# A loop over runs of an expert layer: two wide blocks for three narrow ones, and semaphores set back in stages

## The chip, the cores and the metric

The kernel runs on one core of one Trainium2 chip. A core has five engines with instruction streams of their own: TensorE (PE: matmuls, with its weight loads listed as PEld), VectorE (DVE), ScalarE (ACT), GpSimd (POOL, which here issues the indirect DMAs) and SyncE (SP, which issues the other DMAs). They wait for one another and for DMAs through semaphores. Matmuls read the on-chip memory SBUF and write PSUM, a small memory from which DVE and ACT read the results. The metric is the device time of one execution, in microseconds (us); less is better. Times of the kernel before: median 9008.61 us of 3 runs, from 9005.31 to 9009.49.

## The reference

`x` is (4, 1024, 1024) f32, that is 4096 tokens of 1024 numbers. Two residual stages follow each other. The second holds nearly all the time: a layer of 8 experts, of which every token uses the two that a router gives the highest probability.

```python
x = x + xattn(layernorm(x), ctx_512, W_k, b_k, ln_gamma, ln_beta)   # cross-attention, softmax weights
x = x + ffn(layernorm(x), gate_w, w1, w2, w3)

def ffn(x, gate_w, w1, w2, w3):            # E=8, D=1024, M=3584
    x_flat = x.reshape(-1, d)
    router_probs = softmax(x_flat @ gate_w)
    topk_w, topk_idx = top_k(router_probs, 2);  topk_w /= sum(topk_w)
    x_rep_sort = take(x_flat, argsort(topk_idx.reshape(-1)) // 2)
    group_sizes = bincount(topk_idx, length=8)
    h = silu(ragged_dot(x_rep_sort, w1, group_sizes)) * ragged_dot(x_rep_sort, w3, group_sizes)
    out_sort = ragged_dot(h, w2, group_sizes)
    # back to the order of the tokens, weighted with topk_w and summed over the two
```

With the inputs given, the router sends 984, 991, 1080, 994, 1047, 1004, 1046 and 1046 tokens to the eight experts, 8192 in all. The kernel learns these numbers only while it runs.

## The kernel before

A first stage works through the tokens in tiles of 128: attention, layer norms, router. It writes the normalised tokens to `h_d` and the first residual sum to `out` in device memory, and enters each token into the slot table `id_d` of its two experts. Then it counts: the table RUNS holds the cases that the code has been built for, a number of blocks and their width, such as `(3, 352)` for up to 1056 tokens in three blocks of 352. Small DVE operations (L523 to L564) pick for every expert the first case that holds its tokens and fill `run_e`, `run_s` and `run_k` (expert, first slot, case) and `run_n` (number of runs).

The loop `tc.For_i(0, n_run)` (L896) makes one run at a time: here eight, one for each expert. SP loads the run's expert and first slot into registers, every engine loads its case, and `tc.Switch` (L900) branches to the code of that case. At the end of an iteration all engines stop, the semaphores are set back, and the next iteration begins.

Within `run`, a block of `width` tokens goes through two phases, both by a scheme of Strassen and Winograd: seven products of half-size factors in place of eight. So a matmul has n = width/2 moving columns.

- Phase 1: for 14 pairs of column tiles of w1 and w3, load a tile (L600, 1 MB), form three sums and one difference of its quarters on DVE (`weight_sums`, L632 to L635), 28 matmuls (L825), and `combine` (L666 to L672), which adds the seven products together out of PSUM. Then `silu` (L836), the product of both (L837) into `g`, and `token_sums` (L650 to L652), which adds the sums T1 to T4 that phase 2 needs, so that `g` has seven parts for each of 14 steps.
- Phase 2: for four quarters `q` of the output columns, load w2 in units of 8, 8, 6 and 6 tiles, sum them, and make 14×7 matmuls (L864) that accumulate in PSUM; `combine` puts the result into `y`.

That is 14×2×28 + 4×98 = 1176 matmuls for a block. The order of TensorE is that of the source (`manual_schedule`); the other engines' instructions are ordered by the scheduler.

Small work is put between the matmuls through the list `late`, from which one step is taken after every group in phase 1 and after every seven matmuls in phase 2. `tokens_out` transposes a piece of `y` (L774), adds it, weighted, to `acc` (L776), and after the last quarter scatters `acc` to `out` (L780); what is left of the last quarter of a run is done in the next run, or behind the loop (`leftover`). `tokens_in` transposes the next block's tokens (L743) into `x` (copies L749, L751). The rows are gathered by indirect DMAs (L699): `rows` from `h_d`, `acc` from `out`. `load_first` brings the next run's first tiles of w1 and w3 into tiles of their own (`w1a`, `w3a`), at the start of the last block's phase 2.

Weight tiles rotate through three buffers (`wp`). In PSUM, `banks()` takes four of six rotating buffers for the seven products of a group, and the transposes rotate through two more. There are three row tiles of 128 tokens (RT = 3), each with a tile in `rows` and one in `acc`.

Of the kernel before, what the change touches and what calls it, by code (L numbers as in the profile page):

```python
# [22 lines left out]
RUNS = [(1, 192), (1, 376), (2, 288), (2, 376), (3, 288)]  # L23
RUNS += [(3, w) for w in range(320, 377, 8)]
# [10 lines left out]
def kernel(  # L35
# [540 lines left out]
    with ExitStack() as st:  # L576
        fst = st.enter_context(tc.tile_pool(name="fst", bufs=1))
        wp = st.enter_context(tc.tile_pool(name="wp", bufs=3))
        hp = st.enter_context(tc.tile_pool(name="hp", bufs=1))
        gp = st.enter_context(tc.tile_pool(name="gp", bufs=2))  # L580
        ip = st.enter_context(tc.tile_pool(name="ip", bufs=2))
        ps = st.enter_context(tc.tile_pool(name="ps", bufs=6, space=PSUM))
        pst = st.enter_context(tc.tile_pool(name="pst", bufs=2, space=PSUM))
# [4 lines left out]
        W2K = [8, 8, 6, 6]  # L588
# [3 lines left out]
        XW = RT * P  # L592
        assert all(w // 2 <= NM and w <= XW for _, w in RUNS)


        T1, B11, B12, B21, B22, T2, T4 = range(7)
        T3 = B12
# [9 lines left out]
        def load(wf, ex, k0, kn, c0):  # L607
            t = wp.tile([P, KD, QW], F32, tag="w", name="wt")
            weights(t, wf, ex, k0, kn, c0)
            return t  # L610

        def factors(t, kn, halves, s):

            n = kn // 2
            if halves:
                v = t[:, :kn, :].rearrange("p (i h) c -> p i h c", h=2)
                lo, hi = v[:, :, 0, :], v[:, :, 1, :]
            else:
                lo, hi = t[:, :n, :], t[:, n:kn, :]
            s1, s2, s4 = (s[:, j, :n, :] for j in range(3))  # L620

            return dict(
                p1=lo[:, :, :P], p2=hi[:, :, :P], p3=s4, p4=hi[:, :, P:], p5=s1, p6=s2,
                p7=lo[:, :, P:],
            )

        def weight_sums(t, kn, halves, s=None):
            if s is None:
                s = wp.tile([P, 3, HK, P], F32, tag="s", name="ws")
            f = factors(t, kn, halves, s)  # L630
# [4 lines left out]
            nc.vector.tensor_tensor(a21, a11, a21, ALU.subtract)  # L635
            return f

        RIGHT = dict(p1=B11, p2=B21, p3=B22, p4=T4, p5=T1, p6=T2, p7=T3)
        BANK = dict(p1=(0, 0), p2=(1, 0), p6=(1, 1), p5=(2, 0), p7=(2, 1), p3=(3, 0), p4=(3, 1))
        ENDS = ["p1", "p6", "p7", "p4"]  # L640
# [4 lines left out]
        def token_sums(v, n):  # L645

            def two(a, b):
                return v[..., a : b + 1 : b - a, :]

            nc.vector.tensor_tensor(two(T1, T3), two(B12, B22), two(B11, B12), ALU.subtract)  # L650
            nc.vector.tensor_tensor(v[..., T2, :], v[..., B22, :], v[..., T1, :], ALU.subtract)
            nc.vector.tensor_tensor(v[..., T4, :], v[..., B21, :], v[..., T2, :], ALU.subtract)  # L652

        def banks():
            return [ps.tile([P, N], F32, tag="ps", name=f"ps{i}") for i in range(4)]

        def combine(pp, n, c, wide):

            def pair(t):
                return t[:, : 2 * n].rearrange("p (a b) -> p a b", b=n)  # L660

            def twice(v):
# [3 lines left out]
            nc.scalar.copy(p1s, pp[0][:, :n])  # L666
            nc.vector.tensor_tensor(pair(c), pair(pp[1]), twice(p1s), ALU.add)  # L667
            vu = gp.tile([P, 2, n], F32, tag="vu", name="vu")
            nc.vector.tensor_tensor(vu, pair(pp[2]), twice(c[:, n : 2 * n]), ALU.add)  # L669
            mid = c[:, n : 2 * wide - n].rearrange("p (a b) -> p a b", b=wide - n)[:, :, :n]  # L670
            nc.vector.tensor_tensor(mid, pair(pp[3]), vu, ALU.add)  # L671
            nc.vector.tensor_tensor(  # L672
                c[:, wide + n : wide + 2 * n], pp[2][:, :n], vu[:, 1, :], ALU.add
            )

# [32 lines left out]
        rd0 = fst.tile([P, RT], I32, name="rd0")  # L708
        rows = [fst.tile([P, D], F32, name=f"rows{s}") for s in range(RT)]
        w1a = fst.tile([P, KD, QW], F32, name="w1a")  # L710
        w3a = fst.tile([P, KD, QW], F32, name="w3a")
        s1a = fst.tile([P, 3, HK, P], F32, name="s1a")
# [6 lines left out]
        acc = [fst.tile([P, D], F32, name=f"acc{s}") for s in range(RT)]  # L719
        for a in acc:  # L720
            nc.vector.memset(a, 0.0)
# [3 lines left out]
        def load_rows(s0):  # L725
            load_ids(ids0, s0)
            where_from(rd0, ids0)
            for s in range(RT):
                gather(rows[s], h_d, rd0, s, P)

        def load_first(i):
            ex = expert(i)
            load_rows(first_slot(i))
            weights(w1a, w1f, ex, 0, KD, 0)
            weights(w3a, w3f, ex, 0, KD, 0)

        def tokens_in():


            def step(s, h):  # L740
                pt = pst.tile([P, N], F32, tag="pt", name="pt_h")
                for k in range(HK):
                    nc.tensor.transpose(  # L743
                        pt[:, ts(k, P)], rows[s][:, ts(HK * h + k, P)], ident
                    )
                src = pt.rearrange("p (a b) -> p a b", b=P)
                dst = x[:, ds(HK * h, HK), ts(s, P)]
                if h % 2:
                    nc.vector.tensor_copy(dst, src)  # L749
                else:  # L750
                    nc.scalar.copy(dst, src)  # L751
# [14 lines left out]

        def tokens_out(ids, split, q, y):
# [3 lines left out]
            def step(s, r):  # L771
                pt = pst.tile([P, N], F32, tag="pt", name="pt_y")
                for d in range(2):
                    nc.tensor.transpose(pt[:r, ts(d, P)], yv[:, d, ds(s * P, r)], ident)  # L774
                part = acc[s][:r, ts(q, QW)]
                nc.vector.scalar_tensor_tensor(  # L776
                    part, pt[:r, :QW], ids.bitcast(F32)[:r, s, 1:2], part, ALU.mult, ALU.add
                )
                if q == DQ - 1:
# [3 lines left out]
                        in_=acc[s][:r, :],  # L783
# [7 lines left out]
        def leftover():  # L791
            return tokens_out(ids1, [P] * RT, DQ - 1, y1)

        def run(i, ex, s0, blocks, width):
            n = width // 2
            split = [min(P, width - c) for c in range(0, width, P)]

# [9 lines left out]
            for b in range(blocks):  # L807
                ids, rd = take_ids()
                last = b == blocks - 1
                if not last:  # L810
                    load_rows(s0 + (b + 1) * width)
                g = hp.tile([P, NI, 7, n], F32, tag="g", name="g")
                for i2 in range(NI):
                    cs = []
                    for wf, wa, tag in ((w1f, w1a, "c1"), (w3f, w3a, "c3")):
                        t = load(wf, ex, 0, KD, i2 * QW) if b or i2 else wa
                        if t is w1a:
                            left = factors(w1a, KD, False, s1a)
                        else:
                            left = weight_sums(t, KD, False)  # L820
                        pp = banks()
                        for p in ORDER if b or i2 else EARLY:
                            bk, half = BANK[p]
                            for k in range(HK):
                                nc.tensor.matmul(  # L825
                                    pp[bk][:, ts(half, n)], left[p][:, k, :],
                                    right[p][:, k, :],
# [8 lines left out]
                    nc.scalar.activation(c1, c1, AF.Silu)  # L836
                    nc.vector.tensor_tensor(  # L837
                        g[:, i2, B11 : B22 + 1, :].rearrange("p a b -> p (a b)"), c1, c3,
                        ALU.mult,
                    )  # L840
                    token_sums(g[:, i2, :, :], n)

                if last:
                    load_first(i + 1)
# [6 lines left out]
                for s, r in enumerate(split):  # L851
                    gather(acc[s][:r, :], of, rd, s, r)
                for q in range(DQ):
                    pp = banks()
                    i2 = 0
                    for kn in W2K:
                        t = load(w2f, ex, 2 * i2, kn, q * QW)
                        left = weight_sums(t, kn, True)
                        for k in range(kn // 2):
                            for p in ORDER:  # L860
                                bk, half = BANK[p]


                                nc.tensor.matmul(  # L864
                                    pp[bk][:, ts(half, n)], left[p][:, k, :],
                                    g[:, i2, RIGHT[p], :],
                                    start=(i2 == 0 and half == 0),
                                    stop=(i2 == NI - 1 and p in ENDS),
                                )
                            i2 += 1  # L870
                            if late and i2 > 1:
                                late.pop(0)()
                    if last and q == DQ - 1:
# [5 lines left out]
                    if q == 1:  # L879
                        late += tokens_in()  # L880

                        def sums():
                            nonlocal right
                            if last:
                                weight_sums(w1a, KD, False, s1a)
                            else:
                                right = token_factors(n)

                        late.append(sums)

        load_first(0)
        for step in tokens_in():
            step()
        weight_sums(w1a, KD, False, s1a)
        n_run = nc.values_load(run_n, min_val=1, max_val=NRUN)
        with tc.For_i(0, n_run) as i:  # L896
# [36 lines left out]
```

## Time and profile before

| view | value |
| --- | --- |
| median of 3 runs | 9008.61 us |
| profiled execution, own time | 9005.26 us |
| its span, first to last instruction | 9003.5 us |
| mean granted TensorE clock | 0.987 |
| first matmul of the loop | 535.38 us |
| start of the first leftover transpose behind the loop | 8988.21 us |
| DVE busy | 5109.8 us, 57% |
| ACT, POOL busy | 8%, 5% |
| DMA | 1236.38 MB, mean 137 GB/s |

Matmuls and weight loads are listed separately and overlap. A row of the profile's groups gives line, engine, operation, the output and input tiles, the shapes, the number of records, then the busy time and the mean length of one record, then the idle time of the engine before them and what ended it. Because matmuls are pipelined, the mean length of a record is more than the time between the starts of two. Records such as `128x176` name 128 partitions by 176 columns, here n = 176. The forms in the loop are n = 164, 168, 176 and 180, for widths of 328, 336, 352 and 360, in three blocks each. Branches and register loads are in the trace but do not count as busy. Loads of weights land 4.7 us (768 KB) and 5.1 us (1 MB) after their issue, in the median.

### The profile page before, as it was taken

To read this page: it belongs to the slowest core of one execution; us is meant where nothing else is said; L and a number is where in the kernel's file an instruction comes from. 1 tells how busy PE (TensorE), PEld (TensorE's weight loads), DVE (VectorE), ACT (ScalarE), POOL (GpSimd) and SP (SyncE) were. 2 spreads that over 40 slices of the span, in tenths; PEclk is the share of its full clock that TensorE was granted. 3 is DMA by queue.
4 is the path that set the end of the run, shared out by engine and by line. 5 is a ranking of instruction groups with operands and counts; after the bars stand their busy time and mean duration, and the time that the engine had idled before them with its cause. 6 is when DMAs were issued, how large, how long until landed. Compare 5 with 4: busy or idle time off the path is not lost. (4 is left out here: it accounts for less than half of the span.)

```text
span 9003.5 us, 140017 instructions
## 1 busy us (share of the span) xinstructions
PE 8812.5 (98%) x59462; PEld 8651.3 (96%) x59463; DVE 5109.8 (57%) x10101; ACT 698.5 (8%) x1528; POOL 412.4 (5%) x496
## 2 busy tenths in 40 slices
PE   8979999999999999999999999999999999999999
PEld 5579999999999999999999999999999999999999
DVE  5665655655655655556556556456565565555554
ACT  3310000000000000000000000000000000000000
POOL 2310000000000000000000000000000000000000
PEclk9989999999999999999999999999999999999999
DMA  3234444444443444444444434444444444434343
GB/s 139 109 132 145 139 147 146 138 149 136 154 130 120 144 135 139 133 139 141 142 134 143 142 124 137 145 131 151 142 145 133 129 140 137 140 129 144 125 140 126
DMA packets 1115213, 1236.38 MB, mean 137 GB/s; under 512 B 35312, under 2 KB 1075184, under 8 KB 1114416
## 3 DMA queue, kind: packets, MB, share of 16 engines
q1 hardware_dynamic: 1081616, 1118.37, 38.3%
q0 software_dynamic: 32656, 107.24, 3.4%
q8 instruction: 501, 8.21, 0.4%
q14 instruction: 296, 2.42, 0.1%
q10 hardware_dynamic: 144, 0.13, 0.0%
HBM read 1155.26 MB, written 73.53 MB: 136 GB/s over the span
## 5 line engine op out<-in xcount | busy, mean ns | idle before, releaser
L825 PE MATMUL ps<-x,wt 128*128 128x168 f32 (+3 forms) x15744 | 2510.6, 309 | 0.0
L825 PEld LDWEIGHTS ps<-x,wt 128*128 128x128 f32 x15744 | 2351.7, 190 | 0.0
L864 PE MATMUL ps<-g,wt 128*128 128x168 f32 (+3 forms) x10752 | 2070.9, 309 | 0.0
L632 DVE TENSOR_TENSOR ws<-wt 128x512 f32<-128x512 f32 (+1 forms) x1040 | 693.7, 667 | 2120.1 <-DMA wt<-in_L_ffn_w_dram 2042.2
L864 PEld LDWEIGHTS ps<-g,wt 128*128 128x128 f32 x10752 | 1691.4, 190 | 0.0
L825 PE MATMUL ps<-xs,ws 128*128 128x168 f32 (+3 forms) x10624 | 1659.2, 309 | 0.0
L864 PE MATMUL ps<-g,ws 128*128 128x168 f32 (+3 forms) x8064 | 1615.3, 309 | 0.0
L825 PEld LDWEIGHTS ps<-xs,ws 128*128 128x128 f32 x10624 | 1579.0, 190 | 0.0
L864 PEld LDWEIGHTS ps<-g,ws 128*128 128x128 f32 x8064 | 1294.7, 190 | 0.0
L667 DVE TENSOR_TENSOR c<-ps,p1s 128x352 f32<-128x352 f32 (+3 forms) x672 | 346.5, 516 | 1030.9 <-PE ps L825 1000.1
L825 PE MATMUL ps<-x,ws 128*128 128x168 f32 (+3 forms) x5312 | 883.2, 309 | 0.0
L825 PE MATMUL ps<-xs,wt 128*128 128x168 f32 (+3 forms) x5248 | 872.5, 309 | 0.0
L825 PEld LDWEIGHTS ps<-x,ws 128*128 128x128 f32 x5312 | 804.0, 190 | 0.0
L825 PEld LDWEIGHTS ps<-xs,wt 128*128 128x128 f32 x5248 | 794.3, 190 | 0.0
L633 DVE TENSOR_TENSOR ws<-ws,wt 128x512 f32<-128x512 f32 (+1 forms) x1040 | 692.0, 665 | 28.4
L635 DVE TENSOR_TENSOR wt<-wt 128x512 f32<-128x512 f32 (+1 forms) x1040 | 685.7, 659 | 0.0
L634 DVE TENSOR_TENSOR ws<-wt,ws 128x512 f32<-128x512 f32 (+1 forms) x1040 | 684.6, 658 | 0.0
L666 ACT COPY p1s<-ps 128x168 f32<-128x168 f32 (+3 forms) x768 | 228.2, 297 | 4658.8 <-PE ps L864 2341.3
L836 ACT ACTIVATE c<-c 128x672 f32<-128x672 f32 (+3 forms) x336 | 261.5, 778 | 2648.0 <-DVE c L671 2626.8
L671 DVE TENSOR_TENSOR c<-ps,vu 128x352 f32<-128x352 f32 (+3 forms) x672 | 344.6, 513 | 28.5 <-PE ps L825 20.8
L669 DVE TENSOR_TENSOR vu<-ps,c 128x352 f32<-128x352 f32 (+3 forms) x672 | 342.3, 509 | 5.7 <-PE ps L825 5.6
L699 POOL DMA_INDIRECT rows<-h_d,rd x75 | 79.7, 1063 | 4880.1 <-DVE ws L633 2278.0
(186 smaller groups left out, 3746.1 us busy)
## 6 DMA issues: line engine op xcount, KB each, us to landing
wt<-in_L_ffn_w_dram SPq DMA_DIRECT2D x848, 1024.0 KB, 5.1
wt<-in_L_ffn_w_dram SPq DMA_DIRECT2D x192, 768.0 KB, 4.7
xt<-in_x_dram SPq DMA_DIRECT2D x32, 512.0 KB, 4.3
out_dram<-x SPq DMA_DIRECT2D x32, 512.0 KB, 2.9
h_d<-hn SPq DMA_DIRECT2D x32, 512.0 KB, 2.6
w1a<-in_L_ffn_w_dram SPq DMA_DIRECT2D x9, 1024.0 KB
w3a<-in_L_ffn_w_dram SPq DMA_DIRECT2D x9, 1024.0 KB
cx<-in_ctx_dram SPq DMA_DIRECT2D x4, 1024.0 KB
```

The costliest lines, as they stand in the source:

```text
L632: nc.vector.tensor_tensor(f["p5"], a21, a22, ALU.add)
L633: nc.vector.tensor_tensor(f["p6"], f["p5"], a11, ALU.subtract)
L634: nc.vector.tensor_tensor(f["p3"], a12, f["p6"], ALU.subtract)
L635: nc.vector.tensor_tensor(a21, a11, a21, ALU.subtract)
L666: nc.scalar.copy(p1s, pp[0][:, :n])
L667: nc.vector.tensor_tensor(pair(c), pair(pp[1]), twice(p1s), ALU.add)
L669: nc.vector.tensor_tensor(vu, pair(pp[2]), twice(c[:, n : 2 * n]), ALU.add)
L671: nc.vector.tensor_tensor(mid, pair(pp[3]), vu, ALU.add)
L699: nc.gpsimd.indirect_dma_start(out=dst, out_offset=None, in_=src, in_offset=bass.IndirectOffsetOnAxis(ap=rd[:n, s : s + 1], axis=0),)
L825: nc.tensor.matmul(pp[bk][:, ts(half, n)], left[p][:, k, :], right[p][:, k, :], start=(k == 0), stop=(k == HK - 1),)
L836: nc.scalar.activation(c1, c1, AF.Silu)
L864: nc.tensor.matmul(pp[bk][:, ts(half, n)], left[p][:, k, :], g[:, i2, RIGHT[p], :], start=(i2 == 0 and half == 0), stop=(i2 == NI - 1 and ...
```

## The change

- RUNS gets up to two blocks, in steps of 4 tokens of width from 480 to 564, in place of up to three in steps of 8. It has 27 cases in place of 13; the largest holds 1128 tokens in both. For the groups above, the widths become 492, 496, 540, 500, 524, 504, 524 and 524, two blocks each.
- RT becomes 5: four row tiles of 128 and one of 64. `acc` is gone; a row tile first takes a token's row from `h_d` and, after it was transposed, that from `out` (`rows_of_out`, issued after each copy). The loads of the next rows move to step RT-1 of phase 1; `tokens_in` moves from behind quarter 1 into quarter 0.
- PSUM: one tile of 512 columns for p1, three tiles of 2×512 for the other six products, each with one buffer, and one buffer for transposes.
- Three weight tiles and three sum tiles, which are named and used in turn, across runs as well. The next run's first two tiles go into this rotation, and are loaded in the last unit of the last quarter.
- `g` keeps four parts for each step (B11, T1, B21, B22). T2, T3 and T4 are formed again in each quarter by `hidden_factors`, two DVE operations for each step, into four rotating buffers. The w2 units are 4, 6, 6, 6, 6, and the last unit of a quarter goes product by product.
- `combine` finishes the part that needs only the second pair before the one (`mid`) that needs the third.
- The loop gets `iteration_sync="staggered"`. In the compiled program the whole Switch is one stage: at its end each engine waits for its own semaphores' final counts (TensorE for its last matmul), then branches; SP waits for all, sets the stage's eight semaphores back and loads its registers, and only then releases the others, which load their case and branch.

```diff
-RUNS = [(1, 192), (1, 376), (2, 288), (2, 376), (3, 288)]
-RUNS += [(3, w) for w in range(320, 377, 8)]
+RUNS = [(1, 192), (1, 376), (1, 564), (2, 376), (2, 432)]
+RUNS += [(2, w) for w in range(480, 565, 4)]
...
-        ps = st.enter_context(tc.tile_pool(name="ps", bufs=6, space=PSUM))
-        pst = st.enter_context(tc.tile_pool(name="pst", bufs=2, space=PSUM))
+        ps1 = st.enter_context(tc.tile_pool(name="ps1", bufs=1, space=PSUM))
+        ps2 = st.enter_context(tc.tile_pool(name="ps2", bufs=3, space=PSUM))
+        pst = st.enter_context(tc.tile_pool(name="pst", bufs=1, space=PSUM))
...
-        W2K = [8, 8, 6, 6]
+        W2K = [4, 6, 6, 6, 6]
+        WR = 3
...
+        ROWS = [P, P, P, P, P // 2]
...
         def banks():
-            return [ps.tile([P, N], F32, tag="ps", name=f"ps{i}") for i in range(4)]
+            one = ps1.tile([P, N], F32, tag="ps1", name="ps1")
+            two = [ps2.tile([P, 2, N], F32, tag="ps2", name=f"ps2_{i}") for i in range(3)]
+            pp = dict(p1=one)
+            for t, (a, b) in zip(two, (("p2", "p6"), ("p5", "p7"), ("p3", "p4"))):
+                pp[a], pp[b] = t[:, 0, :], t[:, 1, :]
...
+            nc.vector.tensor_tensor(c2, qa[:, :, :n], twice(p1s), ALU.add)
             vu = gp.tile([P, 2, n], F32, tag="vu", name="vu")
+            nc.vector.tensor_tensor(vu, qb[:, :, :n], twice(c[:, n : 2 * n]), ALU.add)
             mid = c[:, n : 2 * wide - n].rearrange("p (a b) -> p a b", b=wide - n)[:, :, :n]
...
+                c[:, wide + n : wide + 2 * n], qb[:, 0, :n], vu[:, 1, :], ALU.add
+            )
+            nc.vector.tensor_tensor(mid, qc[:, :, :n], vu, ALU.add)
...
+        def load_first(i, j):
+
+            weights(wts_in[j], (w1f, w3f)[j], expert(i), 0, KD, 0)
...
+        def hidden_factors(v, n):
+
+            t = tp.tile([P, 3, n], F32, tag="t", name="t")
+            t2 = t[:, 0, :]
+            nc.vector.tensor_tensor(t2, v[:, B22, :], v[:, T1, :], ALU.subtract)
+            nc.vector.tensor_tensor(
+                t[:, 1:3, :], v[:, B11 : B21 + 1 : B21 - B11, :],
+                t2.unsqueeze(1).to_broadcast([P, 2, n]), ALU.subtract,
+            )
...
-                    token_sums(g[:, i2, :, :], n)
+                    nc.vector.tensor_tensor(
+                        v[:, T1, :], v[:, B12, :], v[:, B11, :], ALU.subtract
+                    )
+                    if i2 == RT - 1:
+                        assert not late
+                        load_rows(first_slot(i + 1) if last else s0 + width)
...
+                        todo = [
+                            (p, k) for k in range(kn // 2) for p in ORDER
+                        ] if u < len(W2K) - 1 else [
+                            (p, k) for p in ORDER for k in range(kn // 2)
+                        ]
+                        if last and q == DQ - 1 and u == len(W2K) - 1:
+
+                            assert j % WR == WR - 1 == 2
+                            load_first(i + 1, 0)
+                            load_first(i + 1, 1)
+                            late.append(lambda: weight_sums(0, KD, False))
+                        hid = [hidden_factors(g[:, i2 + k, :, :], n) for k in range(kn // 2)]
...
-        with tc.For_i(0, n_run) as i:
+        with tc.For_i(0, n_run, iteration_sync="staggered") as i:
```

In the changed kernel the matmuls of the two phases are on L838 and L894, the transposes on L737 and L783, `mid` on L672, `hidden_factors` on L766 and L767.

## The prediction

> **What bounds the kernel now.** I read the busy times first, then the clock, the chain of waits, TensorE's own waits, and the timeline where TensorE stands still.
>
> ```profile
> PE 8812.5 (98%) x59462; PEld 8651.3 (96%) x59463; DVE 5109.8 (57%) x10101; ACT 698.5 (8%) x1528; POOL 412.4 (5%) x496
> PEclk9989999999999999999999999999999999999999
> ...
> 7944.22 208.84 PE ps L825 x1400
> ...
> 600.00:700.00 100.00, 100.00 (x721) 1.00 0.42 137
> 2650.00:2750.00 100.00, 100.00 (x658) 1.00 0.39 127
> ...
> PE ps L825 <- issue: 67.4, 7, 10.7
> PE ps L825 <- DVE xs L760: 10.9, 1, 10.9
> ```
>
> TensorE is busy 98% at full clock, and the chain is a string of L825 and L864 matmuls with nothing between (third line: start, length, number of records). Each f32 matmul leaves two records, so a block of 1176 matmuls leaves 2352. The two 100-us windows (busy, records, clock) lie in phase 1 of a run with n=164 and one with n=180: 138.7 and 152.0 ns per record, 13.3 ns for 16 columns, which is 1/1.2 ns a column. The chain's 1400 records at n=176 last 149.17 ns each, 146.67 of that for columns, which leaves **2.5 ns per record** whatever its width. The last two lines are the run boundaries: seven stops of 10.1 to 10.9 us, 10.3 in the mean without the longest. Apart from them the loop, 535.38 to about 8985.7, is solid: 2352×(4128/1.2+24×2.5)=8232 us of records, where 4128 is Σn over 24 blocks, 126 us of transposes, the boundaries, 1.7 us for the first slow records: together about 8450.
>
> **Fewer and wider matmuls.** The groups of 984, 991, 1080, 994, 1047, 1004, 1046 and 1046 tokens now take two blocks with n=246, 248, 270, 250, 262, 252, 262, 262. Σn falls from 4128 to 4104, records from 56448 to 37632. Columns: 24×2352/1.2=47.0 us less. Fixed cost: 18816×2.5=47.0 less. Sum **−94.1**, leaving 8137.9 us of records. No row has f32 matmuls of n near 260 in this loop; the nearest are in the stage before it:
>
> ```profile
> 53.48 13.90 PE L298 MATMUL pm_o<-pT,kv 128*128 128x512 f32 x32
> 67.21 1.04 PE L217 MATMUL pt<-ident,hn 128*128 128x128 f32 x8
> ...
> 73.29 7.14 PE L250 MATMUL pm_kv<-wkT,cT 128*128 128x256 f32 x32
> 80.27 1.02 PE L323 MATMUL sim<-kvT,oT 128*128 128x512 f32 x2
> ```
>
> From start to next start, 32 records of 512 columns take 13.73 us, 429.1 ns each: 2.4 above columns/1.2. The 256-column ones take 6.98 us, 218.1 each: 4.8 above. L250 has waits on a DVE bias-add in its rows, and the widths on both sides (164 to 180, and 512) agree on 2.4 to 2.5, so I take 2.5. With 4.8 the records would cost 37632×2.3=87 us more; with 2.4, 4 less. Transposes: 10 in-steps and 5 out-steps per quarter on wider blocks, 127 against 126 us: +1.
>
> **The boundary.** The chain shows today's 10.3 us as about 5.3 us until every engine has stopped and is reset, and 4.71 us until the first matmul:
>
> ```profile
> 7905.54 0.51 DVE L671 TENSOR_TENSOR y<-ps,vu 128x352 f32<-128x352 f32 x1
> 7910.56 4.71 issue
> 7915.27 5.05 PE L825 MATMUL ps<-x,w1a 128*128 128x176 f32 x16 [10.09 <-issue]
> 7920.11 1.97 PE L825 MATMUL ps<-x,s1a 128*128 128x176 f32 x8
> ```
>
> The trace's branch records: TensorE's loop branch takes 4.64 us and starts 2.3 us before its last matmul ends (the sequencer runs ahead); after the reset there is the load of run_k and a switch branch of 3.38 us. In the staged program the whole Switch is one stage. TensorE has to wait for its own last matmul before its loop branch (0.45+4.64=5.1 us, nothing hidden), SyncE then makes the stage's eight resets and the run_e and run_s loads, about 1.5 us, which stood beside others before, and only then come run_k (0.9) and the switch branch (3.4): about 11.1 us, +0.8 for each of seven: **+6**. Bounds: if only run_k and the switch branch stay in sight, 4.3 us, −42; if DVE's own 3.5-us branch and SyncE's work stand in series, 15.3 us, +35. I take +6, by the compiled order. The first 16 records take 4.84 us instead of 2.39; the gap stays, so that loss does: 0. Queued behind SyncE's wait are all loads, but the next run's first two weight tiles (load_first in the last unit) and its rows (unit 4 of phase 1) are issued before it.
>
> The Trainium skill ("Runtime: NRT & Kernel Launch", section Instruction fetch mechanics) says that instructions are fetched in order, in blocks of 256, and that a taken branch out of the window waits for a fetch from memory. The 3.38 and 4.64 us are what this trace shows of it. By that rule no kind of reset removes the two branches, and the staged loop would gain nothing; my sum says the same by the rows.
>
> **One PSUM buffer each, and DVE's new work.** Before, six buffers rotate under groups of four. Now p1 has one, the three pairs one each, the transposes one. DVE also forms T2 to T4 anew in each quarter.
>
> ```profile
> L632 DVE TENSOR_TENSOR ws<-wt 128x384 f32<-128x384 f32 x192 | 107.2, 558 | 583.8 <-DMA wt<-in_L_ffn_w_dram 583.8
> L667 DVE TENSOR_TENSOR c<-ps,p1s 128x352 f32<-128x352 f32 x252 | 132.1, 524 | 431.1 <-PE ps L825 420.2 <-ACT p1s L666 10.8
> L837 DVE TENSOR_TENSOR g<-c,c 128x704 f32<-128x704 f32 x126 | 112.3, 892 | 3.9
> L672 DVE TENSOR_TENSOR c<-ps,vu 128x176 f32<-128x176 f32 x252 | 84.4, 335 | 0.1
> ```
>
> Here 335, 524 and 892 ns at 176, 352 and 704 elements are 0.15 us and 1.05 ns an element. At n=262 an operation on n costs 0.43, one on 2n 0.70. A quarter then holds 9.7 us of weight sums, 14×1.08=15.2 of T's (pairs overlap a little), 2.4 of combine and 2.0 of row additions: 29.3 of TensorE's 44.4 us, so DVE has room, and the first T's of a block are made in phase 1. The tight spot is a quarter's end: the last products are p3 and p4, their `mid` operation can start only then, behind one 0.70-us T operation that began up to 0.4 us earlier; it is done 1.2 to 1.3 us after the last matmul. The next quarter writes p3 as its sixth product, 5×0.44=2.2 us in. So 0.9 us is to spare, and 1.1 us at the end of phase 1 and for the second pt_y. What removes the cover is a late weight tile (768 KB land in 4.7 us, median; a unit has 9.3). I put **+5** for such events, bounds 0 and 40 (half of 80 ends by 1 us).
>
> The Trainium skill ("Perfetto Trace Analysis", section Optimizing Tensor Performance) asks for PSUM banks that rotate between groups so that evacuation lies beside the next group; this change gives the rotation up. By the rule each of 80 ends would show its 1.2 us, about 96 us; by the rows above, none.
>
> **Front and tail.** Before the loop: 14 more table steps of three DVE operations at 0.076 us pitch, +3.2; two more row tiles, so ten transposing steps with a single PSUM buffer at about 1.5 us each (1.05 for the 64-row tile) instead of six with two, +8.1; three 1.22-us memsets of acc go, −3.7 of which little was on the path; entry to the staged loop +2. I take **+10** (3 to 16). Behind it five leftover scatters stand in place of three:
>
> ```profile
> 8989.89 1.01 POOL L780 DMA_INDIRECT out_dram<-acc,ids  x1 [138.04 <-DVE acc L776]
> 8994.04 0.99 POOL L780 DMA_INDIRECT out_dram<-acc,ids  x1 [3.14 <-DMA out_dram<-acc,ids]
> 8998.17 0.98 POOL L780 DMA_INDIRECT out_dram<-acc,ids  x1 [3.13 <-DMA out_dram<-acc,ids]
> ```
>
> Each waits for the one before, 4.14 us apart: +8.3, less 0.5 for the shorter combine: **+8** (4 to 9). The scatters' and gathers' places inside the loop move, but lie under matmuls.
>
> **Sum.** −94+1+6+5+10+8 = −64. From the profiled execution's 9005.26 us (span 9003.5 and 1.8 around it) that gives 8941.3; the median shown is 3.35 higher, so **8945 us**, 0.7% less.
>
> **Rivals.**
> (1) The staging does free the boundary: TensorE's branch runs while others finish. For it: 5.3 of 10.3 us today is waiting for the others. Against: in the compiled order TensorE waits for its own end, and SyncE releases everyone. At 4.3 us instead of 11.1, 48 less: 8897. Chance 0.08.
> (2) **DVE decides at the quarter ends.** Place: `mid` behind a T operation, before the next quarter's p3, at 64 ends. For: DVE at 66% in phase 2, weight sums that wait for DMA in the same queue (583.8 us of such waits today), no spare buffer. Against: 0.9 us to spare. Beyond it each 1 us late costs 64; from 1.0 us a quarter the gain is gone, at 1.6 us it is 102: 9047, slower. Chance 0.12.
> (3) Records of 250 to 270 columns cost 4.8 ns beyond their columns, like L250's: +87, 9031. Against: the widths around. Half of it gives 8988. Chance 0.10.
> My own case, 8910 to 8985: 0.70.
>
> **How the numbers follow.** A measurement of this kernel can tell about 0.2%, 18 us, from nothing. Below 8990.6 lie my case, (1) and a part of (3): 0.78 faster. Within 0.2%: 0.09, parts of (2) and (3). Slower: 0.13. The range goes from 8910, where the boundary gives back half of (1), to 9000, with half of (3) or a stall of 0.8 us a quarter; about 0.06 is left below and 0.14 above.
>
> **What would show it.** L838 and L894 at n=262 with 220.8 ns between starts in an unbroken chain; 37632 records; TensorE's boundary waits near 11 us seven times; first loop matmul near 545.7; five scatters at the end. Wrong, if TensorE's waits show `mid` (L672) or L766/L767 at quarter ends, if a pitch of 223 ns shows, or if the boundary is far from 11 us.

## The result, and the profile after

The changed kernel takes **8961.9 us** (median of 5 runs, 8959.18 to 8963.86), against 9007.42 us for the kernel before (5 runs). The ratio is 0.9949, with a 95% interval of 0.9935 to 0.9964: 0.5% faster, 45 us. The forecast was 8945 us, a gain of 64 us.

The profiled execution has a span of 8957.5 us, 46.0 less than before. First the busy times and the clock on its page, then two windows of 100 us in phase 1 (busy time, records, clock, DMA share, GB/s) for n=270 and n=262, then TensorE's waits in the loop (total, times, longest):

```profile
PE 8734.8 (98%) x40738; PEld 7530.2 (84%) x40739; DVE 4824.1 (54%) x8820; ACT 666.7 (7%) x1170; POOL 438.2 (5%) x512
PEclk9979999999999999999999999999999999999999
...
2650.00:2750.00 100.00, 100.00 (x441) 1.00 0.35 109
7950.00:8050.00 100.00, 100.00 (x455) 1.00 0.35 109
...
PE ps L838 <- issue: 96.5, 8, 12.7
PE pt_h L737 <- ACT x L746: 3.2, 5, 0.7
PE ps L838 <- DVE c L665: 0.8, 2, 0.5
```

TensorE is still the bound: 98% busy, in windows without a gap. The first wait is the run boundaries; without the 9.5 us of the first entry, 87.0 us at seven boundaries, 12.4 each (before: 72.6 and 10.4). The other waits of the loop are about 1 us. At a quarter's end DVE keeps its time. In this piece of the timeline (start, length, engine, line) the new quarter begins at 8888.78 with p1 and p2:

```profile
8888.56 0.70 DVE L767 TENSOR_TENSOR t<-g,t 128x524 f32<-128x524 f32 x1
8888.78 1.05 PE L894 MATMUL ps<-g,w 128*128 128x262 f32 x4
...
8889.18 0.70 DVE L672 TENSOR_TENSOR y<-ps,vu 128x524 f32<-128x524 f32 x1
...
8890.99 0.38 PE L894 MATMUL ps<-g,s 128*128 128x262 f32 x1
```

`mid` (L672) stands behind one T operation (L767), as foreseen, and ends at 8889.88, 1.10 us into the quarter. p3, which needs its banks, comes at 8890.99. The median over the 48 quarter ends inside phase 2 is 1.07 us to spare; at two of them it is 0.4 and 0.05 us.

Outside the loop the first transposes are slow, and there are five scatters at the end, of which the first two and the last are shown:

```profile
522.72 1.08 PE L737 MATMUL pt_h<-ident,rows 128*128 128x128 f32 x4 [25.36 <-DMA w<-in_L_ffn_w_dram]
524.52 1.11 PE L737 MATMUL pt_h<-ident,rows 128*128 128x128 f32 x4 [0.72 <-ACT x L746]
526.42 1.11 PE L737 MATMUL pt_h<-ident,rows 128*128 128x128 f32 x4 [0.78 <-DVE x L742]
...
548.87 5.72 PE L838 MATMUL ps<-x,w 128*128 128x246 f32 x16 [9.54 <-issue]
```

```profile
8937.03 1.03 POOL L790 DMA_INDIRECT out_dram<-rows,ids  x1 [145.16 <-DVE rows L785]
8941.24 0.99 POOL L790 DMA_INDIRECT out_dram<-rows,ids  x1 [3.18 <-DVE rows L785]
...
8953.59 0.92 POOL L790 DMA_INDIRECT out_dram<-rows,ids  x1 [3.10 <-issue]
```

From the starts of all TensorE records of both traces the whole difference can be laid out. "Records" is what n/1.2 + 2.5 ns gives for every matmul record; what is left of each interval is sorted by its place.

| term, us | before | after | difference | forecast |
| --- | --- | --- | --- | --- |
| matmul records in the loop | 8232.0 | 8137.9 | −94.1 | −94 |
| transposes in the loop, with the standing around them | 126.8 | 139.4 | +12.5 | +1 |
| seven boundaries, beyond a record | 73.7 | 88.1 | +14.4 | +6 |
| slow records behind them and behind the entry | 18.8 | 17.1 | −1.7 | 0 |
| other standing in phase 1 and 2 | 0 | 1.8 | +1.8 | +5 |
| up to the loop's first matmul | 535.4 | 548.9 | +13.5 | +10 |
| behind the last | 16.8 | 24.3 | +7.6 | +8 |

But for rounding the rows add up to the two spans, and their differences to −46.0.

### The profile page after: what moved, and what is told of

It is laid out like the page before. It is cut to its first block, busy times and chain, and to the rows that moved or that the text cites. A ratio compares the mean times of both kernels' runs of the same rounds, so it can differ in the third digit from the quotient of the medians.

```text
span 8957.5 us, 99534 instructions
## 1 busy us (share of the span) xinstructions
PE 8734.8 (98%) x40738; PEld 7530.2 (84%) x40739; DVE 4824.1 (54%) x8820; ACT 666.7 (7%) x1170; POOL 438.2 (5%) x512
## 5 line engine op out<-in xcount | busy, mean ns | idle before, releaser
L838 PE MATMUL ps<-x,w 128*128 128x262 f32 (+5 forms) x10752 | 2487.9, 381 | 97.3 <-issue 96.5
L838 PEld LDWEIGHTS ps<-x,w 128*128 128x128 f32 x10752 | 2043.4, 191 | 387.9 <-issue 99.4
L838 PE MATMUL ps<-xs,s 128*128 128x262 f32 (+5 forms) x7168 | 1625.9, 379 | 0.0
L838 PEld LDWEIGHTS ps<-xs,s 128*128 128x128 f32 x7168 | 1355.0, 189 | 195.1
L894 PE MATMUL ps<-g,s 128*128 128x262 f32 (+5 forms) x3584 | 1026.1, 379 | 0.0
L894 PE MATMUL ps<-t,w 128*128 128x262 f32 (+5 forms) x3584 | 1025.0, 379 | 0.0
L894 PE MATMUL ps<-g,w 128*128 128x262 f32 (+5 forms) x3584 | 904.7, 381 | 0.0
L838 PE MATMUL ps<-xs,w 128*128 128x262 f32 (+5 forms) x3584 | 848.2, 379 | 0.0
L838 PE MATMUL ps<-x,s 128*128 128x262 f32 (+5 forms) x3584 | 848.2, 380 | 0.0
L672 DVE TENSOR_TENSOR c<-ps,vu 128x524 f32<-128x524 f32 (+5 forms) x448 | 309.7, 691 | 914.4 <-PE ps L838 914.4
L894 PEld LDWEIGHTS ps<-g,s 128*128 128x128 f32 x3584 | 680.1, 190 | 95.2 <-DVE y L672 0.2
L838 PEld LDWEIGHTS ps<-x,s 128*128 128x128 f32 x3584 | 680.9, 190 | 94.1
L838 PEld LDWEIGHTS ps<-xs,w 128*128 128x128 f32 x3584 | 678.6, 189 | 96.4
L894 PEld LDWEIGHTS ps<-t,w 128*128 128x128 f32 x3584 | 678.7, 189 | 96.2
L766 DVE TENSOR_TENSOR t<-g 128x262 f32<-128x262 f32 (+5 forms) x896 | 375.4, 423 | 671.4 <-PE ps L894 667.9
L894 PEld LDWEIGHTS ps<-g,w 128*128 128x128 f32 x3584 | 651.4, 190 | 76.6
L767 DVE TENSOR_TENSOR t<-g,t 128x524 f32<-128x524 f32 (+5 forms) x896 | 613.1, 689 | 16.5
L894 PE MATMUL ps<-t,s 128*128 128x262 f32 (+5 forms) x1792 | 513.0, 380 | 0.0
```

The costliest lines, as they stand in the source:

```text
L672: nc.vector.tensor_tensor(mid, qc[:, :, :n], vu, ALU.add)
L766: nc.vector.tensor_tensor(t2, v[:, B22, :], v[:, T1, :], ALU.subtract)
L767: nc.vector.tensor_tensor(t[:, 1:3, :], v[:, B11 : B21 + 1 : B21 - B11, :], t2.unsqueeze(1).to_broadcast([P, 2, n]), ALU.subtract,)
L838: nc.tensor.matmul(pp[p][:, :n], left[p][:, k, :], right[p][:, k, :], start=(k == 0), stop=(k == HK - 1),)
L894: nc.tensor.matmul(pp[p][:, :n], left[p][:, k, :], hid[k][p], start=(i2 + k == 0), stop=(i2 + k == NI - 1),)
```

## The experiments

Eight kernels ran, the first four on one chip, the last four on another; on the first the kernel before had 9007.06 us, on the second 9005.81.

**The plain loop end.** Edit:

```diff
-        with tc.For_i(0, n_run, iteration_sync="staggered") as i:
+        with tc.For_i(0, n_run) as i:
```

> The changed kernel with the plain loop end (all engines stop) in place of the staged one; nothing else differs. Theory: the staged end costs more than the stop, 12.6 us against 10.5 us at each of seven boundaries, because the loop branch starts only when all engines have reported their end and SyncE's resets and register loads then stand in series with the switch branch; the entry to the first iteration is longer too (9.85 us against 5.0 us). So about 15 us and 4 us less: 8943 us, boundaries near 10.5 us. Rival: the wider blocks (DVE's later end, the longer code of 27 cases) make the boundary longer, not the staging: then 8962 us and 12.6 us stay. Second rival: the staging did hide something that the stop shows: over 8970 us.

Measured: 8945.1 us (8941.12 to 8946.56), ratio to before 0.9931 (0.9914 to 0.9947); 16.8 us less than the changed kernel. TensorE's waits:

```profile
PE ps L838 <- issue: 77.6, 8, 10.8
```

The seven boundaries sum to 73.0 us in place of 88.1, as in the kernel before (73.7). So the staged end costs the changed kernel 15 us, and wide blocks cost the boundary nothing. The 4 us foreseen for the entry are not in the time: the first loop matmul starts at 549.0, with staging at 548.9. The trace shows the entry itself 3.8 us shorter (TensorE stands 5.8 us ahead of that matmul in place of 9.5), but the rows landed later, with the first transposes at 526.64 in place of 522.72. Why they came later is open.

**The staged end in the kernel before**, the same line the other way.

> The kernel before with the staged loop end alone. Theory that staging itself is the cost: boundaries of 12.6 us in place of 10.5 us and a longer entry, 9007 + 15 + 4 = 9026 us. Rival, that the blocks and the code of the change are to blame: 9007 us, boundaries near 10.5 us. Second rival, that the old kernel gains by it because its own end is a different one: under 9000 us.

Measured: 9017.52 us (10 runs), ratio 1.0013 (1.0003 to 1.0023): slower by 10 us, not by 19. The boundary, in the timeline:

```profile
7913.25 0.46 PE L864 MATMUL ps<-g,wt 128*128 128x176 f32 x2
7924.77 4.98 PE L825 MATMUL ps<-x,w1a 128*128 128x176 f32 x16 [11.06 <-issue]
```

Here the seven boundaries sum to 79.8 us, 0.9 each above the plain end. TensorE stands 11.3 us ahead of the first loop matmul in place of 5.7, but its rows had come sooner, so that this matmul is only 3.0 us later.

The branch records of the traces show why a boundary costs less here than in the changed kernel. An engine has reported when it has branched back and counted a semaphore up. Means of the seven boundaries, in us from the start of TensorE's last record:

| event | before | before, staged | changed, plain end | changed |
| --- | --- | --- | --- | --- |
| TensorE's loop branch starts | −1.9 | −1.8 | −3.2 | 1.5 |
| DVE's loop branch starts | 1.1 | 1.2 | 1.1 | 1.4 |
| TensorE has reported | 3.0 | 3.1 | 1.8 | 5.3 |
| the last engine has reported | 4.7 | 4.8 | 4.5 | 5.8 |
| TensorE loads run_k | 6.2 | 6.7 | 6.0 | 8.2 |
| TensorE's switch branch starts | 6.9 | 7.8 | 6.8 | 8.9 |
| first matmul | 10.7 | 11.6 | 10.6 | 12.8 |

The loop branches of TensorE and DVE at one boundary of the kernel before with staging, and at one of the changed kernel with the matmul behind it:

```profile
L896 PEldq COMPARE_BRANCH  x1: 4684/4684/4684, 7911.6 to 7911.6; - x1
L896 DVEq COMPARE_BRANCH  x1: 70/70/70, 7914.6 to 7914.6; - x1
...
L916 DVEq COMPARE_BRANCH  x1: 70/70/70, 7862.7 to 7862.7; - x1
L916 PEldq COMPARE_BRANCH  x1: 3875/3875/3875, 7862.8 to 7862.8; - x1
7873.92 5.92 PE L838 MATMUL ps<-x,w 128*128 128x262 f32 x16 [12.23 <-issue]
```

In the first three kernels DVE reports last at all seven boundaries: its branch stands behind `mid`, and its next record comes some 3.5 us later. TensorE's branch is hidden beside that. With staging in the kernel before, SyncE's loads and resets stand between the last report and the switch branch, 3.0 us in place of 2.2, which is nearly all of the 0.9 us. In the changed kernel the compiled loop puts the body's final waits ahead of the branch. All engines first wait until DVE has come to the end of the body, behind `mid`, and then all five branch, at 1.3 to 1.8 us. The last of them, which is DVE three times, TensorE twice and SyncE twice, has reported at 5.8 us, 1.0 later than DVE alone in the kernel before with staging. From there to the load of run_k it is 2.4 us in place of 1.9; the switch branch follows 0.4 sooner behind that load. That the common branch is most of the other 1.2 us was read from these traces and not tried by itself.

**Steps of 8 in place of 4.**

```diff
-RUNS += [(2, w) for w in range(480, 565, 4)]
+RUNS += [(2, w) for w in range(480, 569, 8)]
```

> The changed kernel with widths in steps of 8, not 4: n becomes 248, 248, 272, 252, 264, 252, 264, 264, so the columns of a pass over all blocks are 4128, exactly those of the kernel before, in 37632 records. Theory (time per record = columns/1.2 + 2.5 ns): 24 columns x 2352 / 1.2 = 47 us more, 2.5 us less in front for 10 or 11 fewer table steps: 9006 us, that is the kernel before's time within 5 us. Rival, that the fixed part per record is larger at these widths (4.8 ns, as in the 256-column rows of the stage in front): columns would be a smaller part of the gain, but the difference between the two step sizes would still be 47 us; the pitch at n=264 tells: 222.5 ns against 224.8 ns.

Measured: 9005.32 us, ratio 0.9998 (0.9988 to 1.0007), as foreseen within 1 us. The same window as above, now n=264:

```profile
7950.00:8050.00 100.00, 100.00 (x454) 1.00 0.38 119
```

454 records in 100 us are 220.3 ns at the least, against the 222.5 expected; 454 counts the records cut by the window's edges. The intervals between starts settle it: for n=246 to 272 they exceed n/1.2 by 2.5 ns to within 0.1 ns. So the two sizes of the forecast's main term stand: 24 columns of 4128 are worth 47 us, about the whole net gain of the change. The 47 us from fewer records are just eaten by its costs.

**Three blocks in the changed kernel**: the table of cases of the kernel before, `ROWS = [P, P, P]`, all else as changed. The load of the next rows is written for two blocks, so that the third block works on the second's tokens again; the amount of work is that of three blocks.

> The changed kernel with the table of cases of the kernel before (three blocks, n = 164 to 180) and three row tiles: T2 to T4 formed again in each quarter, single PSUM buffers and the staged end stay. Theory: records +94 us (8232 against 8138), transposes back to 126 us (-12), front -10, tail -7, boundary as now: 8962 + 94 - 12 - 10 - 7 = 9027 us; DVE's work of a quarter is then 25.5 us of 29.3 us, tight but enough. Rival, that DVE's new work and the single buffers are only affordable under wide blocks: at 87% of the quarter DVE falls behind, 72 to 96 quarter ends with 0.5 us or more each, over 9065 us, and TensorE's waits name DVE.

Measured: 9094.39 us (9086.71 to 9101.12), ratio 1.0095 (1.0078 to 1.0112). That is the rival's side. TensorE's waits on DVE, and a DVE wait:

```profile
PE ps L838 <- DVE c L669: 23.5, 22, 2.1
PE ps L894 <- DVE y L672: 7.3, 34, 0.2
...
1609.43 0.69 DVE L633 TENSOR_TENSOR s<-w 128x512 f32<-128x512 f32 x1 [6.69 <-DMA w<-in_L_ffn_w_dram]
```

The intervals between records give two places. At 72 quarter ends 33 us are lost, 23 ahead of p3 and 10 already ahead of p5: `mid` now ends 1.76 us after the end (median), and p3 would come at 1.49. In phase 1's third step, where `load_rows` stands in this variant, 31 us: a weight tile came late, as the DVE row shows, and the combines queued behind its sums. That tile was issued at 1598.74 and used 10.7 us later, with the three gathers of `load_rows` beside it; loads of 1 MB land 5.0 us after their issue in this kernel's median. That the gathers delay it was not tried. The boundaries rise to 96.4 us. So the second rival's mechanism at the quarter ends is real, and the wide blocks are what hides it: a product lasts 0.44 us at n=262 and 0.30 at n=176.

**`mid` made twice, and three times**, in phase 2:

```diff
             nc.vector.tensor_tensor(mid, qc[:, :, :n], vu, ALU.add)
+            if wide > n + n:
+                for _ in range(1):      # 2 in the other kernel
+                    nc.vector.tensor_tensor(mid, qc[:, :, :n], vu, ALU.add)
```

> The changed kernel with mid, the last operation of combine, made a second time in phase 2 only (it writes the same values again). It holds the third pair of PSUM banks longer. In the changed kernel's trace mid is done 1.10 us after a quarter's end and the next quarter writes p3 at 2.17 us: 1.07 us to spare. With one T operation between, the second mid ends at about 2.4 us. Theory that the quarter's end is covered by those 2.17 us and by nothing else: 0.25 us at each of 48 quarter ends inside a block's phase 2, 12 us, and 0.65 us at each of seven boundaries, 5 us: 8962 + 17 = 8979 us. Rival, that more cover is there (the products reach the bank later than the trace says): 8967 us. Second rival, that DVE is the bound of a quarter already: each extra operation would cost its full 0.7 us, 64 x 0.7 = 45 us: 9007 us.

> As the one before, mid made three times in phase 2. The third ends near 3.45 us after the quarter's end, 1.28 us behind the need. Theory: 48 x 1.28 = 61 us, and 1.3 us at seven boundaries, 9 us: 9032 us, with TensorE's waits naming the extra mid. Rival of more cover: under 9000 us. Rival that DVE bounds the quarter: twice the cost of the kernel with two, about 9050 us.

Measured: 8974.78 us, ratio 0.9966 (0.9952 to 0.9980), and 9039.66 us, ratio 1.0038 (1.0024 to 1.0052): 12.9 and 77.8 us above the changed kernel, where 17 and 70 were expected. With three, TensorE's waits and one quarter's end:

```profile
PE ps L897 <- DVE y L675: 51.7, 48, 1.7
...
8968.07 0.70 DVE L675 TENSOR_TENSOR y<-ps,vu 128x524 f32<-128x524 f32 x1
8968.68 0.42 DVE L769 TENSOR_TENSOR t<-g 128x262 f32<-128x262 f32 x1
8968.91 0.68 PE L897 MATMUL ps<-g,s 128*128 128x262 f32 x2 [1.06 <-DVE y L675]
```

All 48 quarter ends wait, p3 starts right behind the third `mid` at 3.42 us (median) in place of 2.17. With two, `mid` ends at 2.06 and p3 is only 0.04 us late (2.21). So the slack at a quarter's end is the 1.07 us that the changed trace shows; the first 0.7 us of lateness cost 5.3 us in phase 2 and the next cost 58.

**Two PSUM buffers for the transposes ahead of the loop**, with the plain end:

```diff
+                if two and h % 2:
+                    pt = ps1.tile([P, N], F32, tag="ps1", name="pt_h1").rearrange(
+                        "p (a b) -> p a b", b=P
+                    )
+                else:
+                    pt = pst.tile([P, 4, P], F32, tag="pt", name="pt_h")
```

> The kernel with the plain loop end (8945 us) and, ahead of the loop alone, two PSUM buffers in turn for the ten transposing steps (the bank of p1 is free there). Theory: the steps stand 1.8 to 1.9 us apart because each waits for the copy of the one before; with two buffers about 1.0 us, 10 x 0.8 = 8 us less: 8937 us, first loop matmul near 541 us. Rival, that copies or row gathers set the pace and not the buffer: within 2 us of 8945.

Measured: 8935.33 us (8933.35 to 8938.15), ratio 0.9921 (0.9905 to 0.9938). TensorE ahead of the loop:

```profile
525.72 3.49 PE L742 MATMUL pt_h<-ident,rows 128*128 128x128 f32 x16 [25.74 <-DMA w<-in_L_ffn_w_dram]
529.99 1.06 PE L742 MATMUL pt_h<-ident,rows 128*128 128x128 f32 x8 [0.79 <-DMA rows<-h_d,rd]
...
540.58 4.85 PE L843 MATMUL ps<-x,w 128*128 128x246 f32 x11 [6.30 <-issue]
```

Steps now follow each other until the gathers hold them, and the copies do so only once, for 0.24 us. The first loop matmul is 8.4 us earlier than with the plain end alone, and the time 9.8 less.

**Five row tiles of 128 as well** (`ROWS = [P, P, P, P, P]`).

> As the one before, and five row tiles of 128 in place of four and one of 64. In the changed kernel's trace each transposing step of 64 rows costs 0.24 us of standing still around it beside its matmuls of 77 ns in place of 109. Theory: 32 such steps, 7.7 us of standing less, 4.1 us of longer transposes more: 3.6 us less, 8933 us. Rival, that the longer gathers of the last tile come late or that the standing comes with the fifth step whatever its rows: 8937 us or more.

Measured: 8933.85 us (8928.41 to 8934.98), ratio 0.9917 (0.9901 to 0.9934), the fastest kernel of the study. Whether it beats the one before it is not settled: 1.5 us lie within the spread, and the loop in the two traces is 0.7 us shorter (8367.8 against 8368.5), not 3.6. The standing at the 64-row steps is gone, and the transposes with what stands around them take 4.7 us less, somewhat more than foreseen. But 3.2 us more of standing elsewhere in the two phases and 1.5 us more of slow records behind the gaps take most of it back.

## Why the prediction was right, and where it was off

The forecast was right in direction and in its main term, and 17 us too low: the main term gave 94 us as foreseen, and the side terms cost 48 us in the trace in place of 30.

- **Fewer and wider matmuls: right.** −94.1 us, as forecast. The choice between the two nearby rows, 2.5 ns of fixed cost from the 512-column row or 4.8 ns from the 256-column one, decided 87 us; the loop's records have 2.5. The 4.8 was a mean over one odd interval: of the 31 intervals inside the 256-column row 29 are 215 or 216 ns, which is columns/1.2 + 2.5, and one is 288. The third rival is refuted.
- **Boundary: right in sign, mis-sized.** +14.4 in place of +6. The step that failed is "TensorE has to wait for its own last matmul before its loop branch (0.45+4.64=5.1 us, nothing hidden)". It waits for all engines first; all branch together, and the last has reported at 5.8 us. SyncE's part then takes 2.4 us in place of 1.5, and from run_k to the first matmul it is 4.6 in place of 4.3: 12.8 us, where the prediction's terms add up to 10.9. The reading of the kernel before was off too: TensorE's branch is hidden there, and it is DVE's that ends the stop. The first rival, that staging frees the boundary, is refuted by the run without staging, which was 16.8 us faster.
- **Transposes: mis-sized.** +12.5 in place of the +1 of "127 against 126 us". There are 1224 records in place of 1152, 7.9 us at 109 ns. And the 32 steps of 64 rows in the loop are not cheaper but dearer than steps of 128: 0.59 us each in place of 0.44, 4.8 us in all.
- **Single PSUM buffers and DVE's new work: right.** 0.9 us were forecast to be spare at a quarter's end, 1.07 were; standing was +1.8 in place of +5. The runs with extra `mid` show that this slack is the real bound, and the run with three blocks that it would be gone with narrow blocks. The second rival thus named a real mechanism with too high a price here.
- **Front: nearly right.** +13.5 in place of +10. The ten transposing steps took 11.3 us more than the six before (forecast 8.1): one behind a single PSUM buffer costs 1.8 to 1.9 us, not 1.5. The entry took 3.8 us more (forecast 2), and the first step came 1.7 us earlier.
- **Tail: right.** +7.6 against +8, five scatters 4.14 us apart. The loop before ended at 8986.7 us, not at the 8985.7 that the prediction read; no term rests on it.

Against the kernel before, then, columns gave 47 us and fewer records 47; the boundary took back 14, the transposes 13, front and tail 21.

## What to carry to other kernels

When an engine runs at its pitch without a gap, count records and columns: the fixed part per record, read from several widths of the same loop, predicted 94 us, one per cent of the time, to 0.1 us, and the mean of a nearby row of another stage would have misled. A loop end that looks like waiting can be a chain of taken branches and register loads; taking the stop away helps only if those move too, so read for every engine, and not for the busiest alone, where its branch starts against its last work, and which one reports last. Slack that hides an evacuation scales with the length of a matmul: the same single buffers cost next to nothing at the quarter ends with n = 246 to 270, and 33 us with n = 164 to 180.

## What was not expected of the hardware

Four transposes of 64 rows among matmuls are dearer than four of 128. The record ahead of them stands 94 ns longer, their own starts are 112, 63, 62 and 152 ns apart, and the record behind stands 104 ns longer: 0.59 us in place of 4 × 109 ns. A taken branch of TensorE at a boundary costs 3.3 to 5.2 us in all kernels that ran, and the 10 to 14 us of each boundary are mostly two branches in series, the loop branch of the engine that reports last and TensorE's switch branch, with resets and register loads between. Behind every gap the first records are slow, about twice their time: 10 to 21 of them at n = 164 to 180 and 7 to 15 at n = 246 to 272, so that a gap costs 1.5 to 3.1 us more at either width.
